# Two layers of a relational graph network on one core: own products per chunk in place of four chunks at once, and rows copied by ScalarE as well as by SyncE

## The chip, the cores and the metric

The kernel runs on one core of a Trainium2 chip. The core has five engines that each work through their own list of instructions in order: TensorE (PE in the profile; its weight loads are shown apart as PEld), VectorE (DVE), ScalarE (ACT), GpSimd (POOL) and SyncE (SP). [...] The metric is the device time of one execution in microseconds (us); lower is better. The kernel before took 22690.96 us (median of three runs, 22663.02 to 22782.8).

## The reference

There are 50,000 nodes with 128 features each, 850,000 edges (800,000 drawn at random in both directions, and one loop per node), 16 relations. Edges come sorted by their target node. One layer is

```python
W = jnp.einsum('rb,bio->rio', w_comp, basis)          # 16 matrices from 8 bases
seg = dst * N_REL + rel
agg = jax.ops.segment_sum(h[src], seg, num_segments=N_ENT * N_REL)
msg = jnp.einsum('nri,rio->no', agg.reshape(N_ENT, N_REL, -1), W)
out = jax.nn.relu(msg + h @ loop_w + bias)
```

Two such layers follow each other, and the result is `layernorm(x + layer2(layer1(x)))`. The bulk of the data traffic is `h[src]`: 800,000 rows of 512 bytes per layer, at random places.

## The kernel before, in words

**Chunks.** The edges that are not loops are laid out in 625 chunks (`C`) of 10 tiles (`K`) of 128 edges, in the order of their target nodes. For every layer the function `chunked` walks the chunks in one long unrolled program. For a tile, 128 source rows are fetched into an SBUF tile `g`, and one matmul (L1023) multiplies them by `hot`, a matrix that VectorE makes (L913) out of the relation weights and the edges' places among the tile's 12 possible targets. Five tiles fill one PSUM bank `pa`; ScalarE copies it to `aT` (L1031, `aT<-pa`, two copies per chunk). There are two `pa` banks.

**Own products.** `aT` holds, for each of 8 bases, 120 target slots of the chunk. It has to be multiplied by the bases. Before, this is done for `BATCH = 4` chunks together: `slots_of_batch` runs 8 matmuls with 480 columns (L754) into `ps`, ScalarE copies the result out (`by_slot`, L760), four matmuls transpose it into `po` (L764), and VectorE spreads each chunk's part over four node positions (`spread_out`, L742). The last chunks (from `ALONE`) go one by one through `slots` (L732).

**Nodes.** `to_nodes` (L796) adds the spread slots to groups of 512 nodes, which are summed in PSUM banks `pn`; this happens `LAG = 6` chunks after the chunk's own matmuls. `from_itself` makes the part of a group that comes from its own loop (L695, L710, L717, L725), and `finish` adds both, applies the nonlinearity and stores the group.

**Fetching rows.** Two paths bring rows. Nearly all tiles come by an indirect gather on GpSimd (L206), one instruction for 128 rows, issued two chunks ahead (`FETCH`) into one of five buffers (`GATHERS`). In every fifth chunk (`BY_HAND = 5`; chunks 9, 14, ... 624, that is 124 per layer) the last tile is instead copied row by row: `row_by_row` loads the 128 offsets from DRAM (`row_at`, L842), SyncE reads them into registers, 32 at a time (L851), and issues one DMA of 512 bytes for each row (L859). The generator starts `BY_HAND + EARLY = 8` chunks ahead of use and is advanced one step after every tile, 45 steps for 128 rows.

**What sets the order.** The program order of PE, POOL, DVE and ACT is the order of the source, held by a manual schedule. The function `beside` puts pieces of the other work after each tile. SyncE's order is left to the scheduler, which follows the source closely. So SyncE issues, in one list: the 128 rows, the `row_at` loads, `rel` (L625: the relations of the next four chunks, on which VectorE waits at L632), `h_own` (L685), `lrel`, `xw`, and the stores of finished groups (L821, L826). In the built program the DMAs issued by SyncE carry one of eight completion semaphores in turn, and a DMA waits until the one that last used its semaphore has landed.

Of the kernel before, what the change touches and what calls it, by code (L numbers as in the profile page):

```python
# [72 lines left out]
BATCH = 4  # L73
BY_HAND = 5
EARLY = 3
OFFSETS = 32
LAG = BATCH + 2
# [8 lines left out]
def tile_rgcn_resnorm(  # L86
# [33 lines left out]
    assert D == P and N >= P and edges.shape[0] == 1 and AT * NR == P and PER * NB * WN <= BANK and AT * PER * NB == WEIGHTS and PER == HALF and S <= P and C >= 4 and M > 0 and N % C == 0 and N % J == 0 and J * D == BANK and C % BATCH == 1 and C > 4 * BATCH and RUN - LK // 2 == LIVE and C <= RUN and 2 * C <= NG * P and N <= 1 << 16 and E % ROW == 0  # L120
# [10 lines left out]
    ROW_AT = dram.tile([2 * C, P], I32, name="ROW_AT")  # L131
# [310 lines left out]
    def rows_of(j, pool):  # L442
# [36 lines left out]
        row_at = pool.tile([P, LIVE], F32, name="real").bitcast(I32)[:, :P]  # L479
        nc.vector.tensor_scalar(row_at[:m], srcf[:m, LIVE - P :], float(N - 1), float(4 * D), op0=OP.min, op1=OP.mult)  # L480
        nc.sync.dma_start(ROW_AT[r0 : r0 + m], row_at[:m])
# [63 lines left out]
    def count_up(pool):  # L545
        last = 5 * NG + len(ROWS)
        off = pool.tile([P, RUN], F32, name="k_f")[0:1, :C]
        even = pool.tile([P, RUN], F32, name="loop_f")[0:1, :C]
# [48 lines left out]
    def chunked():  # L597
        with (
# [7 lines left out]

            ALONE = C - BATCH - 1

# [12 lines left out]
            def weights(c, n):  # L621
# [9 lines left out]
                is_rel = hp.tile([P, LIVE], F32, name="is_rel", bufs=1)  # L631
# [14 lines left out]
            def loop_weights(g, n):  # L646
# [14 lines left out]
                is_rel = rel.bitcast(F32)  # L661
                for h in range(2):
                    nc.vector.tensor_scalar(is_rel[:m, h, :], rel[:m, h, :], its_rel1[:m], None, op0=OP.is_equal)  # L663
                    if h == 0:
                        yield
                po = ps_o.tile([P, BANK], F32, name="po")
                of = po[:, : J * T * NB].rearrange("p (j t) -> p j t", j=J)
                for j in range(J):
                    for h in range(2):
                        nc.tensor.matmul(  # L670
                            of[:, j, :],
                            is_rel[:m, h, :].rearrange("k (p j) -> k p j", j=J)[:, :, j],
                            EACH[n][:m, :T, :].rearrange("k t b -> k (t b)"),
                            start=h == 0,
                            stop=h == 1,
                        )
# [4 lines left out]
            def from_itself(g, of, n):  # L681

                m = nodes(g)
                h = sb.tile([P, J, D], F32, name="h_own", bufs=1)
# [43 lines left out]
            def slots(c, k, aT, n):  # L728
# [7 lines left out]
                yield spread_out(c, ps[:, :D])  # L736

            def spread_out(c, of):

                k = ks(c) * WN  # L740
                st = sb.tile([P, J, D], F32, name="slots", bufs=BATCH)
                nc.vector.tensor_tensor(  # L742
                    st[:k],
                    of[:k, None, :].to_broadcast([k, J, D]),
                    which[:k, c, :, None].to_broadcast([k, J, D]),
                    op=OP.mult,
                )
                return st

            def slots_of_batch(c, aT, st, n):  # L750

                ps = ps_s.tile([P, BANK], F32, name="ps")
                for b in range(NB):
                    nc.tensor.matmul(  # L754
                        ps[:, : BATCH * S], BASIS[n][:, b, :], aT[:, b, :], start=b == 0, stop=b == NB - 1
                    )
                    if b < NB - 1:
                        yield
                by_slot = sb.tile([P, BATCH * S], F32, name="by_slot", bufs=1)
                nc.scalar.copy(by_slot, ps[:, : BATCH * S])  # L760
                yield
                po = ps_o.tile([P, BANK], F32, name="po")
                for q in range(BATCH):
                    nc.tensor.transpose(po[:S, q * P : (q + 1) * P], by_slot[:, q * S : (q + 1) * S], ident)  # L764
                    if q == 1:
                        yield
                for q in range(BATCH):
                    st[c + q] = spread_out(c + q, po[:, q * P : (q + 1) * P])
                    if q == 1:
                        yield  # L770
                yield
# [61 lines left out]
            behind = []  # L833

            def by_hand(c):

                return ks(c) == K and c >= BY_HAND + EARLY and c % BY_HAND == BY_HAND - 1

            def row_by_row(c, of):

                row_at = hp.tile([1, P], I32, name="row_at")
                nc.sync.dma_start(row_at, ROW_AT[2 * c + 1 : 2 * c + 2])  # L842
                to = hp.tile([P, D], F32, name="by_hand")
                byte = of.bitcast(U8).rearrange("n d -> (n d)")
                yield to
                steps = BY_HAND * (K - 1)
                for step in range(steps):
                    for e in range(step * P // steps, (step + 1) * P // steps):
                        if e % OFFSETS == 0:
                            with tc.issue_after(behind[-1]) if behind else ExitStack():  # L850
                                _, offsets = nc.values_load_multi_w_load_instructions(  # L851
                                    row_at[:, e : e + OFFSETS],
                                    engines=[mybir.EngineType.SP],
# [5 lines left out]
                        behind[:] = [nc.sync.dma_start(row, byte[None, ds(offsets[e % OFFSETS], 4 * D)]).ins]  # L859
# [39 lines left out]
            for n, of in enumerate((x, H1)):  # L899
# [21 lines left out]
                def sum_up(c):  # L921
                    at = c % BATCH * S
                    for st[c] in slots(c, ks(c), aTs[c // BATCH][:, :, at : at + S], n):
                        yield

                def added_in(c):

                    if c < ALONE + 2:
                        return [c - LAG] if c >= LAG else []
                    at = ALONE - BATCH + 2 * (c - ALONE - 2)  # L930
# [323 lines left out]
```

## Time and profile before

| | |
|---|---|
| median of three runs | 22690.96 us |
| the profiled execution: its time, its span | 22663.02 us, 22661.2 us |
| PE, weight loads (PEld) busy | 11605.0 us, 7642.6 us |
| POOL busy | 11614.3 us |
| DVE busy, ACT busy | 6712.8 us, 1902.9 us |
| mean granted TensorE clock | 0.717 |
| gathers (L206) | 2 x 6126 |
| row copies (L859) | 2 x 15872 |
| mean DMA rate | 46 GB/s |

The profiled execution is the fastest of the three runs, 28 us (0.1%) under the median. In a line of the profile, `L859` is the line of the kernel, `by_hand<-H` the tile written and the one read, `x15872` the number of instructions, and a wait is listed as total us, number of times, longest. SyncE has no busy time in the profile's own count, since issuing DMAs is not counted as busy; what it does must be read from the starts of its instructions.

### The profile page before, as it was taken

To read this page: it belongs to the slowest core of one execution; us is meant where nothing else is said; L and a number is where in the kernel's file an instruction comes from. 1 tells how busy PE (TensorE), PEld (TensorE's weight loads), DVE (VectorE), ACT (ScalarE), POOL (GpSimd) and SP (SyncE) were. 2 spreads that over 40 slices of the span, in tenths; PEclk is the share of its full clock that TensorE was granted. 3 is DMA by queue.
4 is the path that set the end of the run, shared out by engine and by line. 5 is a ranking of instruction groups with operands and counts; after the bars stand their busy time and mean duration, and the time that the engine had idled before them with its cause. 6 is when DMAs were issued, how large, how long until landed. Compare 5 with 4: busy or idle time off the path is not lost. (4 is left out here: it accounts for less than half of the span.)

```text
span 22661.2 us, 191120 instructions
## 1 busy us (share of the span) xinstructions
PE 11605.0 (51%) x45072; PEld 7642.6 (34%) x45072; DVE 6712.8 (30%) x11506; ACT 1902.9 (8%) x3706; POOL 11614.3 (51%) x12285
## 2 busy tenths in 40 slices
PE   4545444544455554554555555555545555455555
PEld 2333333333333333333333333333333333333333
DVE  3333333333222222222222222222222222222222
ACT  0000000000000000000000000000000000000000
POOL 4544544545455554554555555555545555555554
PEclk7767677777677777776767777777767777777777
DMA  2111111111111111111111111111111111111111
GB/s 58 52 49 50 49 49 45 48 49 50 45 44 46 44 43 43 43 47 41 45 44 46 45 47 45 47 46 44 46 43 48 46 45 47 44 46 46 44 48 41
DMA packets 597898, 1048.67 MB, mean 46 GB/s; under 512 B 242858, under 2 KB 320422, under 8 KB 596762
## 3 DMA queue, kind: packets, MB, share of 16 engines
q0 software_dynamic: 395616, 810.55, 13.7%
q1 hardware_dynamic: 197930, 224.36, 3.1%
q8 instruction: 368, 6.03, 0.1%
q14 instruction: 768, 6.29, 0.1%
q10 hardware_dynamic: 3216, 1.45, 0.0%
HBM read 962.43 MB, written 72.95 MB: 46 GB/s over the span
## 5 line engine op out<-in xcount | busy, mean ns | idle before, releaser
L206 POOL DMA_INDIRECT g<-H,src x6126 | 5791.7, 945 | 5388.5 <-PE pa L1023 2718.1
L206 POOL DMA_INDIRECT g<-in_x_dram,src x6126 | 5796.8, 946 | 5111.4 <-PE pa L1023 2627.1
L1023 PEld LDWEIGHTS pa<-hot,g 128*128 128x128 f32 x24504 | 4553.1, 236 | 4871.2 <-issue 3484.1
L1023 PE MATMUL pa<-hot,g 128*128 128x96 f32 x24504 | 4535.0, 313 | 1929.5 <-ACT aT L1031 1107.3
L754 PE MATMUL ps<-aT,basis 128*128 128x480 f32 x4960 | 3081.3, 707 | 1314.3 <-ACT aT L1031 872.4
L796 PE MATMUL pn<-slots,own 120*128 120x512 f32 x4128 | 2507.0, 730 | 2229.8 <-DVE slots L742 1787.1
L710 PE MATMUL po<-basis,hT 128*128 128x512 f32 x3136 | 2035.6, 736 | 2340.5 <-DVE by L717 2107.8
L1031 ACT COPY aT<-pa 128x480 f32<-128x480 f32 x2500 | 1375.6, 558 | 17880.7 <-remote 9150.3
L717 DVE TENSOR_TENSOR by<-po,lw 128x512 f32<-128x512 f32 x1568 | 1069.9, 687 | 4347.4 <-PE po L710 1638.7
L913 DVE TENSOR_TENSOR hot<-fixed,own 128x960 f32<-128x960 f32 x1250 | 1447.1, 1158 | 1699.0 <-remote 1379.3
L796 PEld LDWEIGHTS pn<-slots,own 120*128 120x128 f32 x4128 | 857.0, 236 | 2792.6 <-DVE slots L742 1806.3
L725 DVE TENSOR_REDUCE ls<-by 128x128 f32<-128x1152 f32 (+1 forms) x784 | 1661.9, 2120 | 34.6 <-DVE by L717 0.4
L632 DVE TENSOR_SCALAR is_rel<-rel,its_rel 128x640 f32<-128x640 uint8 x314 | 176.9, 563 | 4458.7 <-DMA rel<-REL 4277.5
L754 PEld LDWEIGHTS ps<-aT,basis 128*128 128x128 f32 x4960 | 924.1, 231 | 1375.4 <-ACT aT L1031 899.6
L710 PEld LDWEIGHTS po<-basis,hT 128*128 128x128 f32 x3136 | 565.2, 226 | 2413.0 <-DVE by L717 2152.7
L742 DVE TENSOR_TENSOR slots<-po,which 120x512 f32<-120x512 f32 x1240 | 780.7, 681 | 1576.4 <-remote 780.6
L906 DVE TENSOR_TENSOR own<-fixed,key 128x120 bf16<-128x120 f32 x1250 | 344.2, 275 | 1887.7 <-remote 1092.0
L764 PE MATMUL po<-ident,by_slot 128*120 128x128 f32 x1240 | 346.6, 375 | 1039.7 <-ACT by_slot L760 798.4
L670 PE MATMUL po<-each,lrel 64*128 64x32 f32 (+1 forms) x800 | 205.8, 416 | 1106.3 <-DVE lrel L663 1052.0
L695 PE MATMUL po<-ident,h_own 128*128 128x128 f32 (+1 forms) x784 | 189.9, 333 | 934.0 <-DMA h_own<-H 606.6
L670 PEld LDWEIGHTS po<-each,lrel 64*128 64x128 f32 (+1 forms) x800 | 193.7, 324 | 1119.1 <-DVE lrel L663 1063.3
L764 PEld LDWEIGHTS po<-ident,by_slot 128*120 128x120 f32 x1240 | 189.7, 193 | 1087.4 <-ACT by_slot L760 831.0
(140 smaller groups left out, 4025.1 us busy)
## 6 DMA issues: line engine op xcount, KB each, us to landing
by_hand<-in_x_dram SPq DMA_DIRECT2D x15872, 0.5 KB
by_hand<-H SPq DMA_DIRECT2D x15872, 0.5 KB
g<-in_x_dram,src POOLq DMA_INDIRECT x6126
g<-H,src POOLq DMA_INDIRECT x6126
rel<-REL SPq DMA_DIRECT2D x312, 80.0 KB
h_own<-in_x_dram SPq DMA_DIRECT2D x97, 256.0 KB
xw<-in_x_dram SPq DMA_DIRECT2D x97, 256.0 KB
H<-ls SPq DMA_DIRECT2D x97, 256.0 KB
```

The lines of the kernel that those rows point to most:

```text
L206: return nc.gpsimd.indirect_dma_start(out=to, out_offset=None, in_=of, in_offset=bass.IndirectOffsetOnAxis(ap=idx, axis=0))
L670: nc.tensor.matmul(of[:, j, :], is_rel[:m, h, :].rearrange("k (p j) -> k p j", j=J)[:, :, j], EACH[n][:m, :T, :].rearrange("k t b -> k (t ...
L710: nc.tensor.matmul(hb[:m], hT[:, j, :m], BASIS[n][:, b : b + few, :].rearrange("p b d -> p (b d)"), start=True, stop=True,)
L717: nc.vector.tensor_tensor(by[:m, b : b + few, :], hb[:m].rearrange("p (b d) -> p b d", d=D), lw[:m, j, g % T, b : b + few, None].to_broadc ...
L725: nc.vector.tensor_reduce(ls[:m, j, :], by[:m].rearrange("p b d -> p d b"), AX.X, OP.add)
L742: nc.vector.tensor_tensor(st[:k], of[:k, None, :].to_broadcast([k, J, D]), which[:k, c, :, None].to_broadcast([k, J, D]), op=OP.mult,)
L754: nc.tensor.matmul(ps[:, : BATCH * S], BASIS[n][:, b, :], aT[:, b, :], start=b == 0, stop=b == NB - 1)
L764: nc.tensor.transpose(po[:S, q * P : (q + 1) * P], by_slot[:, q * S : (q + 1) * S], ident)
L796: nc.tensor.matmul(sums[g], own, of[:k].rearrange("s j d -> s (j d)"), start=c == first(g), stop=c == final(g),)
L913: nc.vector.tensor_tensor(hot[:, : ks(c)], pm[:, c % Q * K : c % Q * K + ks(c), :, None].to_broadcast([P, ks(c), NB, WN]), own[:, : ks(c), ...
L1023: product = nc.tensor.matmul(pa[:, i * NB * WN : (i + 1) * NB * WN], g[:, k + i, :] if k + i < ks(c) - by_hand(c) else handed.pop(c), hot[ ...
L1031: nc.scalar.copy(aT[:, :, place_of + k * WN : place_of + (k + m) * WN].rearrange("d b (i w) -> d i b w", w=WN), pa[:, : m * NB * WN].rearr ...
```

## The change

It has three parts.

1. The batch goes. `slots_of_batch`, `spread_out`, `by_slot` and the transposes are removed; every chunk now runs `slots`: 8 matmuls of 128 columns with `aT` as the weights, and VectorE spreads directly out of `ps`. `aT` becomes a tile per chunk (three buffers), the sum into nodes comes 3 chunks after the chunk instead of 6, and the steps of `beside` are placed accordingly.
2. The row copies have two hands, `HANDS`. SyncE copies a tile in every fifth chunk as before (124 per layer). ScalarE copies one in every sixth chunk (chunks 8, 14, ... 620: 103 per layer), with its own register loads and its own DMA starts on ScalarE's list; the offsets are still fetched by a DMA of SyncE. Those tiles are no longer gathered, so there are 2 x 6023 gathers. Each hand starts `every + 1` chunks ahead (6 for SyncE, 7 for ScalarE), with 45 and 54 steps. `ROW_AT` holds the offsets of two tiles of each chunk.
3. Buffers: `h_own` and `is_rel` get two each, `is_l` is a tile of its own, two small vectors of `count_up` as well.

In the program built from it, ScalarE's row copies stand between its `aT<-pa` copies, about 2.4 after each tile, and the eight completion semaphores are shared by SyncE's and ScalarE's DMAs in the order of the program.

```diff
-BATCH = 4
-BY_HAND = 5
-EARLY = 3
+SP_EVERY = 5
+ACT_EVERY = 6
...
-    ROW_AT = dram.tile([2 * C, P], I32, name="ROW_AT")
+    ROW_AT = dram.tile([2 * C, 2, P], I32, name="ROW_AT")
...
-                is_rel = hp.tile([P, LIVE], F32, name="is_rel", bufs=1)
+                is_rel = hp.tile([P, LIVE], F32, name="is_rel")
...
-                h = sb.tile([P, J, D], F32, name="h_own", bufs=1)
+                h = sb.tile([P, J, D], F32, name="h_own", bufs=2)
...
-                yield spread_out(c, ps[:, :D])
-
-            def spread_out(c, of):
-
-                k = ks(c) * WN
-                st = sb.tile([P, J, D], F32, name="slots", bufs=BATCH)
+                st = sb.tile([P, J, D], F32, name="slots")
                 nc.vector.tensor_tensor(
-                    st[:k],
-                    of[:k, None, :].to_broadcast([k, J, D]),
-                    which[:k, c, :, None].to_broadcast([k, J, D]),
+                    st[: k * WN],
+                    ps[: k * WN, None, :D].to_broadcast([k * WN, J, D]),
+                    which[: k * WN, c, :, None].to_broadcast([k * WN, J, D]),
                     op=OP.mult,
                 )
-                return st
-
-            def slots_of_batch(c, aT, st, n):
-
-                ps = ps_s.tile([P, BANK], F32, name="ps")
-                for b in range(NB):
-                    nc.tensor.matmul(
-                        ps[:, : BATCH * S], BASIS[n][:, b, :], aT[:, b, :], start=b == 0, stop=b == NB - 1
-                    )
...
-                by_slot = sb.tile([P, BATCH * S], F32, name="by_slot", bufs=1)
-                nc.scalar.copy(by_slot, ps[:, : BATCH * S])
...
-            behind = []
+            behind = {}
+            HANDS = ((nc.sync, SP_EVERY, SP_EVERY - 1), (nc.scalar, ACT_EVERY, ACT_EVERY // 2 - 1))
 
             def by_hand(c):
 
-                return ks(c) == K and c >= BY_HAND + EARLY and c % BY_HAND == BY_HAND - 1
-
-            def row_by_row(c, of):
-
-                row_at = hp.tile([1, P], I32, name="row_at")
-                nc.sync.dma_start(row_at, ROW_AT[2 * c + 1 : 2 * c + 2])
-                to = hp.tile([P, D], F32, name="by_hand")
+                if ks(c) < K:
+                    return []
+                return [i for i, (_, every, at) in enumerate(HANDS) if c > every and c % every == at]
+
+            def row_by_row(i, c, of):
+
+                engine, every, _ = HANDS[i]
+                tile_at = 1 - by_hand(c).index(i)
+                row_at = hp.tile([1, P], I32, name=f"row_at{i}", bufs=2)
+                nc.sync.dma_start(row_at, ROW_AT[2 * c + 1 : 2 * c + 2, tile_at])
+                to = hp.tile([P, D], F32, name=f"by_hand{i}", bufs=2)
                 byte = of.bitcast(U8).rearrange("n d -> (n d)")
                 yield to
-                steps = BY_HAND * (K - 1)
+                steps = every * (K - 1)
                 for step in range(steps):
                     for e in range(step * P // steps, (step + 1) * P // steps):
...
-                                    engines=[mybir.EngineType.SP],
+                                    engines=[engine.engine],
...
-                        behind[:] = [nc.sync.dma_start(row, byte[None, ds(offsets[e % OFFSETS], 4 * D)]).ins]
+                        behind[i] = engine.dma_start(row, byte[None, ds(offsets[e % OFFSETS], 4 * D)]).ins
...
-                        for k in range(ks(to) - by_hand(to)):
+                        for k in range(ks(to) - len(by_hand(to))):
...
-                    to = c + BY_HAND + EARLY
-                    if to < C and by_hand(to):
-                        fetching = row_by_row(to, of)
-                        handed[to] = next(fetching)
+                    for i, (_, every, _) in enumerate(HANDS):
+                        to = c + every + 1
+                        if to < C and i in by_hand(to):
+                            fetching[i] = row_by_row(i, to, of)
+                            handed.setdefault(to, {})[K - 1 - by_hand(to).index(i)] = next(fetching[i])
...
                             if k + i < K - 1:
-                                next(fetching, None)
+                                for each in fetching.values():
+                                    next(each, None)
```

## The prediction, made before the changed kernel was run

> **What bounds the kernel now.** I read the page first. No engine is busy for more than half of the span, so the bound must be a wait, or an engine whose work is not counted.
>
> ```profile
> span 22661.2 us, 191120 instructions
> PE 11605.0 (51%) x45072; PEld 7642.6 (34%) x45072; DVE 6712.8 (30%) x11506; ACT 1902.9 (8%) x3706; POOL 11614.3 (51%) x12285
> ```
>
> Then the longest waits over all engines:
>
> ```profile
> POOL g L206 <- PE pa L1023: 5345.2, 368, 50.1
> DVE is_rel L632 <- DMA rel<-REL: 4277.5, 172, 65.9
> PE po L710 <- DVE by L717: 2107.8, 195, 52.6
> ```
>
> GpSimd waits for TensorE to free a buffer, TensorE for VectorE, and VectorE for `rel`, an 80 KB transfer that SyncE issues. With the DMA engines 17% busy it is late because its issue is. The list of SyncE's own waits says that SyncE itself hardly waits for anybody:
>
> ```profile
> SPq L859 <- DMA by_hand<-H: 171.4, 333, 1.4
> SPq L859 <- DMA by_hand<-in_x_dram: 165.9, 338, 1.4
> SPq L826 <- ACT ls L595: 93.3, 21, 20.4
> ```
>
> It always has something to issue: 31,744 row copies in a span of 22,661 us, one per 0.71 us. The instructions of line L859 in two stretches of 20 us (12016 to 12036, then 12085 to 12105) show that the pace depends on what GpSimd does at that time; the two last lines are the busy time of PE, PEld, DVE, ACT and POOL in the same stretches, then the granted clock, the DMA engines' share and GB/s:
>
> ```profile
> L859 SPq DMA_DIRECT2D by_hand<-H x18: 3/230/700, 12017.3 to 12035.0; - x18
> L859 SPq DMA_DIRECT2D by_hand<-H x46: 2/228/263, 12085.4 to 12104.9; - x46
> 12016.00:12036.00 20.00, 9.89 (x55) 8.12 (x53) 2.49 (x4) 1.12 (x2) 15.12 (x17) 0.67 0.21 53
> 12085.00:12105.00 20.00, 0.00 (x0) 0.00 (x0) 0.00 (x0) 0.00 (x0) 0.19 (x1) 0.50 0.02 5
> ```
>
> 46 rows while GpSimd rests and the engines stand still, 18 beside 17 gathers. I counted the starts of both kinds in all 20 us stretches of the trace. Without a gather SyncE starts 44.2 rows (81 stretches), which is 0.4525 us per row with register loads and other transfers included. Each gather then costs SyncE a toll: 0.62 us in stretches with 8 to 11 gathers, 0.66 with 12 to 14, 0.73 with 15 to 17. Over the whole span: 31,744 x 0.4525 = 14,364 us, and the remaining 8,297 us over 12,252 gathers are 0.677 us each, inside that table. SyncE's list is the bound: it has no slack, and the others stop until it catches up. The profiled time is 22,663 us, 1.8 above its span and 28 under the median.
>
> **The change part by part: SyncE.** It keeps its 31,744 rows and 992 register loads (2.1 us each, inside the 0.4525). It loses the toll of 206 gathers and gains 206 `row_at` loads, issued in 0.234 us each (median of L842): 14,364 + 12,046 x 0.677 (8,158) + 48 = 22,570 us. That is 0.4% less than the span and the floor of the changed kernel, unless the toll itself changes.
>
> **ScalarE.** It gets 2 x 103 x 128 = 26,368 row copies and 824 register loads. No row shows ScalarE issuing rows beside gathers. From below: SyncE's record of a row is a move of 0.03 and a DMA of 0.228 us, one per 0.323 at best, so 8,517 us. From above: SyncE's full price, 26,368 x 0.4525 = 11,932, the toll of 8,158, and ScalarE's own busy time of 1,902.9 less 174.5 for the removed `by_slot` copies: 21,818 us. I take the upper value, the nearest row being the same instruction on the other queue. ScalarE is then 96% full, just under SyncE.
>
> **What the new wait does.** The eight completion semaphores now go round both queues, so that neither can start more than about eight transfers past the other's place in the program; a hand holds about four of them. Behind a stopped SyncE stand `rel`, `h_own` and the stores, and behind a stopped ScalarE the `aT<-pa` copies, for which the next `pa` bank and so TensorE wait. A stop of one hand that outlasts four rows of the other (4 x 0.323 = 1.29 us) stops both. In the trace of before 6,683 gaps between SyncE's rows are longer than that, with 4,414 us above 1.29; they cover 58% of the span. Scaled to ScalarE's rows (26,368/31,744) the excess is 3,667 us. From below this costs nothing (both stop together, since the gathers cause both), from above 3,667. I take the part that falls outside SyncE's own long gaps if they fall independently, 42%: 1,547 us.
>
> **Two issuers at once.** No row shows two engines issuing rows. From below zero: they do not meet. From above each SyncE row meets a whole ScalarE record: 31,744 x 0.228 = 7,238 us; and, should the whole price be that of a shared path, 26,368 x 0.4525 = 11,932. I take the chance meeting: ScalarE is inside a 0.228 record for 26% of the time and SyncE then waits half of one, 0.26 x 0.114 x 31,744 = about 960 us.
>
> [...]
>
> **The other edits.** TensorE: the batch cost 3,081.3 (L754) and 346.6 us (L764); the 20,000 matmul records that replace it cost 26.4 us per 160 in the tail of the kernel, so 3,300 us:
>
> ```profile
> L754 PE MATMUL ps<-aT,basis 128*128 128x480 f32 x4960 | 3081.3, 707 | 1314.3 <-ACT aT L1031 872.4 <-issue 439.8 <-DMA g<-in_x_dram,src 1.4
> L764 PE MATMUL po<-ident,by_slot 128*120 128x128 f32 x1240 | 346.6, 375 | 1039.7 <-ACT by_slot L760 798.4 <-issue 228.3 <-DVE at_i L521 6.2
> L732 PE MATMUL ps<-basis,aT 128*120 128x128 f32 x160 | 26.4, 306 | 1.8 <-DVE slots L742 1.8
> ```
>
> That is a draw, and more weight loads (10,000 pairs for 3,720) lie in TensorE's idle half. At the single record's 306 ns it would be 6,120 us, 2,700 more; TensorE's idle 11,056 us hide that, and if SyncE were no longer the bound it would be part of the price. VectorE's spreading keeps its 1,250 instructions (681 against 691 ns). The shorter lag and the second buffers cost nothing while everybody waits for SyncE. SyncE's tile is now asked for 6 chunks ahead instead of 8, and finished one chunk before use; TensorE stood idle for 13.7 us in all before matmuls on such tiles, and a late one would only be another sign of SyncE's lateness.
>
> **Sum.** 22,570 + 1,547 + 960 = 25,077 us, 10.6% above the profiled execution and 10.5% above the median.
>
> **The rivals.** (1) ScalarE's rows are hidden altogether: cheap ones (8,517 us) never stop SyncE, and the floor stands, 22,570. For it: ScalarE is 8% busy now. Against it: its rows stand in one list with copies that wait for TensorE, and the shared semaphores tie SyncE to that list. (2) Both hands go through one path and rows add: 58,112 x 0.4525 + 8,158 + 48 = 34,500. For it: the toll, which shows that transfers of another engine do slow SyncE. Against it: with no gather in flight SyncE runs at 0.323 us per row, which is its own instruction time, and the DMA engines are 2% busy there. (3) The other side, faster: with ScalarE's rows between the copies the gathers come evenly, about 10 in 20 us instead of bursts of 16 and pauses, and the toll falls from 0.677 to the 0.62 of such stretches: 14,364 + 12,046 x 0.62 + 48 = 21,880, 3.6% under the median. It decides where the saved toll (12,046 x 0.057 = 690 us) is more than the coupling, so where that is under 690. Against it: the coupling above is more than three times that.
>
> **How the numbers follow.** The two queues coupled, 25,080: chance 0.60, with a range of its own of 23,200 to 29,860 (a quarter of the two terms above the floor; the whole coupling with half of the 7,238). Hidden, 22,570: 0.16, of which 0.10 within 0.5% of the median, 0.03 on each side; 0.5% is about what this kernel's runs can tell from no change. Shared path: 0.11. Even gathers: 0.13. Faster 0.16, same 0.10, slower 0.74. The range 22,400 to 30,500 leaves out most of the even and of the shared case.
>
> **What would show it.** Right: SyncE's waits for row transfers grow from 337 us to over 1,000; ScalarE's rows have gaps like SyncE's; the waits of VectorE for `rel` shrink, as TensorE now waits for `aT` copies. L732 near 3,300 us busy shows the draw. Wrong: ScalarE's rows at 0.32 us beside gathers, or a pace without gathers under 0.3 us per row for both hands, or TensorE busy for most of the span, would each take the sum apart.

## The result, and the profile after

The changed kernel takes 23,699 us (median of four runs, 23,696 to 23,734), the kernel before beside it 22,686. The ratio is 1.044, 95% interval 1.041 to 1.047: slower, as forecast, by less than half of the forecast 10.5%. The profiled execution has a span of 23,732 us.

The head of the page after, for the changed kernel (busy us, share of the span, instructions):

```profile
span 23732.1 us, 272570 instructions
PE 12540.1 (53%) x58712; PEld 9692.4 (41%) x58712; DVE 6751.1 (28%) x11506; ACT 1789.2 (8%) x3396; POOL 11417.3 (48%) x12079
```

Its waits over all engines, and then SyncE's own (total us, times, longest):

```profile
POOL g L204 <- PE pa L979: 6798.7, 619, 36.6
ACT aT L987 <- DMA by_hand<-in_x_dram: 6202.8, 840, 49.7
PE pa L979 <- ACT aT L987: 3941.9, 763, 44.8
DVE is_rel L630 <- DMA rel<-REL: 3345.5, 154, 56.3
```

```profile
SPq L836 <- DMA by_hand<-H: 807.6, 898, 9.4
SPq L836 <- DMA by_hand<-in_x_dram: 740.2, 828, 9.6
```

Still no engine is busy for long. The `aT` copies now stand behind row transfers on ScalarE's list (the `ACT aT` line), TensorE waits 3,942 us for those copies where it waited 1,107 before, and GpSimd waits for TensorE. The 1,107 is the last number of TensorE's group in the page of the kernel before:

```profile
L1023 PE MATMUL pa<-hot,g 128*128 128x96 f32 x24504 | 4535.0, 313 | 1929.5 <-ACT aT L1031 1107.3
```

VectorE's wait for `rel` shrank from 4,278 to 3,346. SyncE's waits at its rows (L836, was L859) grew from 337 to 1,548 us, and the longest from 1.4 to 9.6. This is what the prediction asked to see, except that TensorE's own products (L732) take 4,106 us and not near 3,300. What it does not show is that two effects of opposite sign lie in the 4.4%, and that this number belongs to one kind of chip.

**One thing is needed to read what follows.** The runs came to several chips, of two kinds. On one kind, where the prediction's trace and the result were taken, the kernel before takes 22,680 to 22,920 us. On the other it takes 15,496 to 15,509 us, with the same instructions. I call them the slow and the quick chips. All ratios below are against the kernel before on the same chip.

| run | chip | us | ratio (95%) |
|---|---|---|---|
| changed kernel | slow | 23,699 | 1.044 (1.041 to 1.047) |
| no_act_hand | slow | 21,730 | 0.958 (0.956 to 0.960) |
| act_twelfth, act_twelfth_again | slow | 25,143, 25,385 | 1.109 (1.106 to 1.111), 1.108 (1.106 to 1.110) |
| act_burst | slow | 24,077 | 1.050 (1.048 to 1.052) |
| sp_burst | slow | 24,015 | 1.049 (1.048 to 1.051) |
| both_sixth | slow | 23,243 | 1.014 (1.012 to 1.016) |
| sp_tenth_act_sixth | slow | 21,870 | 0.954 (0.952 to 0.956) |
| act_alone | slow | 19,477 | 0.852 (0.850 to 0.854) |
| no_hands | slow | 18,878 | 0.825 (0.824 to 0.827) |
| before_no_rows | slow | 18,780 | 0.828 (0.827 to 0.830) |
| before_tenth | slow | 19,206 | 0.847 (0.845 to 0.848) |
| before_three_buffers | slow | 22,748 | 0.994 (0.993 to 0.996) |
| after_again (the changed kernel) | quick | 16,827 | 1.085 (1.083 to 1.087) |
| no_act_one_buffer | quick | 15,502 | 1.000 (1.000 to 1.001) |
| before_lead_six | quick | 15,494 | 1.000 (0.999 to 1.001) |
| before_by_tile | quick | 15,496 | 1.000 (0.999 to 1.001) |
| before_half_gathers, half_gathers_again | quick | 13,925, 13,928 | 0.899 (0.897 to 0.900), 0.898 (0.897 to 0.900) |

### The profile page after: what moved, and what is told of

Same layout as the page of the kernel before. It is cut to its first block, busy times and chain, and to the rows that moved or that the text cites. A ratio compares the mean times of both kernels' runs of the same rounds, so it can differ in the third digit from the quotient of the medians.

```text
span 23732.1 us, 272570 instructions
## 1 busy us (share of the span) xinstructions
PE 12540.1 (53%) x58712; PEld 9692.4 (41%) x58712; DVE 6751.1 (28%) x11506; ACT 1789.2 (8%) x3396; POOL 11417.3 (48%) x12079
## 5 line engine op out<-in xcount | busy, mean ns | idle before, releaser
L979 PE MATMUL pa<-hot,g 128*128 128x96 f32 x24092 | 5177.6, 329 | 6925.6 <-ACT aT L987 3941.9
L979 PEld LDWEIGHTS pa<-hot,g 128*128 128x128 f32 x24092 | 4711.5, 248 | 8696.4 <-issue 4551.1
L732 PE MATMUL ps<-basis,aT 128*120 128x128 f32 x20000 | 4106.2, 341 | 98.6 <-issue 56.4
L737 DVE TENSOR_TENSOR slots<-ps,which 120x512 f32<-120x512 f32 x1250 | 862.4, 690 | 10311.5 <-remote 6830.1
L732 PEld LDWEIGHTS ps<-basis,aT 128*120 128x120 f32 x20000 | 3483.4, 243 | 113.1 <-issue 66.7
L768 PE MATMUL pn<-slots,own 120*128 120x512 f32 x4128 | 2656.5, 768 | 985.4 <-DVE own L751 918.8
L670 PE MATMUL po<-each,is_l 64*128 64x32 f32 (+1 forms) x800 | 205.9, 418 | 835.3 <-DVE is_l L661 821.2
L670 PEld LDWEIGHTS po<-each,is_l 64*128 64x128 f32 (+1 forms) x800 | 193.5, 324 | 850.5 <-DVE is_l L661 835.0
L751 DVE TENSOR_SCALAR own<-col,node 120x128 f32<-120x128 f32 x2064 | 528.6, 293 | 12.1 <-PE pn L768 12.1
L635 PE MATMUL fixed<-each,is_rel 128*128 128x64 f32 x3140 | 465.6, 298 | 99.9 <-issue 97.6
```

The lines of the kernel that those rows point to most:

```text
L635: nc.tensor.matmul(of[:, :, j * NB : (j + 1) * NB], is_rel[:m, j * P : (j + 1) * P], EACH[n][:m], start=True, stop=True,)
L732: nc.tensor.matmul(ps[: k * WN, :D], aT[:, b, : k * WN], BASIS[n][:, b, :], start=b == 0, stop=b == NB - 1)
L737: nc.vector.tensor_tensor(st[: k * WN], ps[: k * WN, None, :D].to_broadcast([k * WN, J, D]), which[: k * WN, c, :, None].to_broadcast([k * ...
L751: nc.vector.tensor_scalar(own[:k], col4[:k], node4[:k, c : c + 1], float(-g * GN), op0=OP.subtract, op1=OP.is_equal)
L768: nc.tensor.matmul(sums[g], own, of[:k].rearrange("s j d -> s (j d)"), start=c == first(g), stop=c == final(g),)
L979: product = nc.tensor.matmul(pa[:, i * NB * WN : (i + 1) * NB * WN], others.get(k + i, g[:, k + i, :]), hot[:, k + i].rearrange("e b w -> ...
```

## The experiments

### Is SyncE's list the bound? before_tenth, before_no_rows

```diff
-BY_HAND = 5
+BY_HAND = 10
```

> The kernel before with SyncE copying a tile in every tenth chunk, not every fifth: 15,872 rows instead of 31,744, 124 more gathers. Theory A (SyncE bounds): 15,872 x 0.4525 + 12,376 x 0.62 = 14,860 us for SyncE, so that GpSimd's pace of 1.25 us per gather (15,470 us) or TensorE takes over: 15,600 to 18,500 us, at most 0.82 of before. If GpSimd's gathers or TensorE were the bound of the kernel before, it would be 22,600 to 23,000, since there is 1% more to gather.

In before_no_rows `by_hand` returns False, and all tiles are gathered:

> The kernel before with no rows by hand at all, every tile gathered: 12,500 gathers. Theory A: GpSimd's 12,500 x 1.25 = 15,625 us are the floor, 15,700 to 18,500 us with what TensorE adds. If the rows by hand relieve the bound, as they would where GpSimd is it: 2% slower than before, about 23,150.

Half of SyncE's rows gone: 0.847. All gone: 0.828. On a slow chip the rows are the bound of the kernel before, and taking them out gains 17%. Both times lie above the 18,500 us at which the expected ranges end, and 18,780 is some 3,150 over 12,500 gathers at 1.25 us, so the rows are not all that keeps this chip from the pace of the gathers. With half of them left SyncE has time to wait for others; its own waits in before_tenth:

```profile
SPq L821 <- ACT ls L820: 1797.2, 69, 61.1
SPq L826 <- ACT ls L595: 1034.7, 72, 28.1
```

In the kernel before the second of these was 93.3 us. A list that waits up to 61 us for a store's data is no bound any more, which fits that the second half of the rows brings only 2%.

### The change without ScalarE's hand, and with half of it: no_act_hand, act_twelfth

```diff
-            HANDS = ((nc.sync, SP_EVERY, SP_EVERY - 1), (nc.scalar, ACT_EVERY, ACT_EVERY // 2 - 1))
+            HANDS = ((nc.sync, SP_EVERY, SP_EVERY - 1),)
```

> The changed kernel without ScalarE's hand: own products per chunk, second buffers and shorter lag stay, 124 tiles per layer by SyncE as before. Theory A (SyncE's list is the bound in both kernels, and what the change adds is SyncE waiting on the completion semaphores that it now shares with ScalarE's transfers): 22,600 to 22,800 us, ratio 0.995 to 1.005. Rival B (TensorE's own products per chunk are the cost): about 23,650. Rival C (rows on ScalarE's list hold up the aT copies and so TensorE): 22,600 to 22,800 as well; runs with fewer ScalarE rows are to tell C from A.

```diff
-ACT_EVERY = 6
+ACT_EVERY = 12
```

> The changed kernel with ScalarE copying a tile in every twelfth chunk, not every sixth: half its rows, 102 more gathers. Theory A: the 1,014 us that the change added are in proportion to the pairs of transfers, so about 23,200 us. Rival B: 23,650, since the own products are as before. Rival C: between, but TensorE's wait for aT copies (3,942 us) halves as well.

None of the expectations had either result. Without ScalarE's hand the changed kernel is 4.2% faster than before, where the prediction had the remaining edits at nothing. So ScalarE's hand costs 23,699 - 21,730 = 1,969 us. Between the two traces the spans differ by 2,005 us, and 1,607 of these are idle time before SyncE's rows (9,127 us against 7,520). The shorter wait of VectorE for `rel` is no sign of the hand, since it is there without it:

```profile
DVE is_rel L630 <- DMA rel<-REL: 3425.1, 156, 61.2
```

With half of ScalarE's rows the hand costs more, not less: some 3,410. SyncE's waits at its rows, first in no_act_hand, then in act_twelfth:

```profile
SPq L836 <- DMA by_hand<-H: 227.3, 463, 1.4
SPq L836 <- DMA by_hand<-in_x_dram: 217.2, 438, 1.7
```

```profile
SPq L836 <- DMA by_hand<-in_x_dram: 1596.3, 749, 45.2
SPq L836 <- DMA by_hand<-H: 1346.6, 732, 17.0
```

444, 1,548 (the changed kernel) and 2,943 us. A wait of 45 us can't be a row's travel: in the quick trace of the changed kernel (after_again, below) a row's data packet starts 0.64 us after the record of its issue ends (median; 0.95 at 95%). It must be a transfer that ScalarE had not issued. I therefore took from each built program which transfer used a semaphore last before each of SyncE's and ScalarE's transfers, and from the trace when that one was issued (idle time of the queue ahead of transfers whose predecessor was not yet issued when the queue was ready):

```
                     SyncE, behind ScalarE     ScalarE, behind SyncE
changed kernel        601 times, 1,410 us      2,001 times, 3,872 us
act_twelfth_again   1,047 times, 4,612 us        368 times,   528 us
act_burst             586 times, 1,666 us      1,669 times, 3,951 us
sp_tenth_act_sixth    297 times,   492 us      1,363 times, 4,402 us
both_sixth            733 times, 1,370 us      2,544 times, 7,389 us
after_again, quick    359 times,   884 us        290 times,   625 us
```

The two hands do hold each other, and what counts is which of them is the later one. In the changed kernel it is mostly SyncE. With half as many rows ScalarE's hand is the later one: SyncE, whose list is the bound, waits 3,202 us more for it, and ScalarE 3,344 less for SyncE. That fits the higher cost of fewer rows: the listed waits of SyncE's rows grew by 1,395 us from the changed kernel to act_twelfth (1,548 to 2,943), the time by 1,444. The repeat, run for another question, gave the same ratio:

> The changed kernel with ScalarE copying a tile in every twelfth chunk and not in every sixth, for a chip without the stops of 0.7 us (kernel before: 15,500 us). SyncE's list takes 13,914 us there when nothing holds it up, and 2,669 us of waits at its rows come on top with both hands at 5 and 6. If the waits go with the number of ScalarE's rows, they halve: 13,914 + 1,335 = 15,250, and the gathers (12,168 x 1.258 + 58 = 15,365) end the time: 0.99. If they go with the number of SyncE's transfers that follow one of ScalarE's on their semaphore (7,454 instead of 10,144): 13,914 + 1,961 = 15,875, 1.025. If half the rows cost more than all, as on the first chips: over 1.085.

### Each hand by itself: no_hands, act_alone

`HANDS = ()`, and `HANDS` with ScalarE's entry alone:

> The changed kernel with neither hand: all 12,500 tiles gathered, own products per chunk. Theory A (SyncE's row copies bound every kernel that has them in every fifth chunk): as the kernel before without rows, 18,780 us, give or take the other edits: 17,900 to 19,200. If TensorE's own products per chunk cost anything by themselves, it shows here, where SyncE no longer hides it: above 19,200.

> The changed kernel with ScalarE's hand alone, a tile in every sixth chunk, and none by SyncE. Theory A (the price of ScalarE's rows is that SyncE's rows wait for them on the shared semaphores): nearly free without SyncE's rows, at most 500 us over the kernel with neither hand. Rival C (ScalarE's rows delay the aT copies, and TensorE with them): 1,000 to 2,000 us over it, as they cost 1,970 beside SyncE's rows (23,700 against 21,730).

0.825 and 0.852: without SyncE's rows beside them, ScalarE's 26,368 rows cost 599 us, against 1,969 beside them. That is a little over the 500 us of theory A, and under the 1,000 to 2,000 of rival C. And no_hands against before_no_rows (0.825, 0.828) says that the own products chunk by chunk cost nothing when there are no rows: TensorE's 20,000 small matmuls are no burden there, although they are busy for 678 us longer than what they replace (4,106 us against 3,081 and 347).

### Changing the order of the rows: sp_burst, act_burst

One hand's steps are taken at the end of a chunk and not after each tile (SyncE's in sp_burst, ScalarE's in act_burst):

```diff
-                                for each in fetching.values():
-                                    next(each, None)
+                                next(fetching.get(0, iter(())), None)
+                    for _ in range(K - 1):
+                        next(fetching.get(1, iter(())), None)
```

> The changed kernel with SyncE's rows of a chunk (about 26) asked for together at the chunk's end instead of three after each tile; ScalarE's stay after each tile. The shared semaphores then change hands between the queues in blocks. Theory A: SyncE's waits for row transfers (1,548 us) fall below 1,000 and the time to 22,300 to 23,300 us. Rival C: the place of ScalarE's rows before the aT copies is as it was, so 23,600 to 23,800.

> The changed kernel, ScalarE's rows asked for nine steps at a time at the end of each chunk (some 21 rows in a row) and not step by step after each tile. In the built program 7,347 of SyncE's transfers follow one of ScalarE's on their semaphore, not 10,144. Chip without the stops: if the waits go with these, 13,914 + 1,933 = 15,850 us, 1.022 of the kernel before, 6% better than the changed kernel there. If the aT copies behind 21 rows (7 us and more) hold up TensorE and so the gathers instead: 1.085 or more. Chip with the stops: under 1.04 by the first, over it by the second.

sp_burst tells nothing: the scheduler put SyncE's list back, and in the built program some 10,100 of SyncE's transfers follow one of ScalarE's on their semaphore, against some 10,150 in the changed kernel. In act_burst it is some 7,350, yet SyncE's waits at its rows are 1,501 us (1,548), and the ratio is 1.050. The number of such pairs does not set the price.

### Less for SyncE with ScalarE's hand kept: both_sixth, sp_tenth_act_sixth

`SP_EVERY` is 6 and 10 in place of 5.

> The changed kernel with SyncE copying a tile in every sixth chunk, ScalarE too. Chip without the stops: SyncE's list 26,368 rows, some 11,740 us, and waits of 2,400 us leave 1,100 us of room under the gathers, 12,108 x 1.258 + 58 = 15,290 us: 0.987 of the kernel before, the fastest of all if the waits stay in that room. If the two hands in step hold each other up more than that: over 1.0. Chip with the stops: about 0.97.

> The changed kernel with SyncE copying a tile in every tenth chunk, and ScalarE one in every sixth as before. Chip without the stops: SyncE's list needs some 7,500 us, so waits of 2,669 us and more have room in it, and the gathers are the bound: 12,190 x 1.258 + 58 = 15,393 us, 0.993 of the kernel before. If it is ScalarE's list or the aT copies behind its rows that hold everything up: over 1.04. Chip with the stops: 0.85 if SyncE's list is the bound there as the other runs say.

I had 0.97 and 0.85 for the slow chip and measured 1.014 and 0.954. In both_sixth ScalarE waits 7,389 us for transfers that SyncE has not issued, the most in the table, and TensorE 6,395 for `aT` copies; why the same period of both hands should do this was not tested. At a tenth SyncE is not the bound: its list has room, as in before_tenth. Beside that run's 0.847 (which has the batch still) ScalarE's hand costs some 0.107 of 22,900, 2,450 us. By the table above ScalarE waits 4,402 us for transfers that SyncE issues late, and SyncE's list waits for VectorE; the `aT` copies stand behind them. The waits of SyncE and of TensorE in sp_tenth_act_sixth:

```profile
SPq L623 <- DVE own L751: 1290.0, 165, 27.7
```

```profile
PE pa L979 <- ACT aT L987: 4938.0, 800, 46.2
```

So the coupling works both ways: a SyncE with room in its list still holds up ScalarE's copies.

### Where does SyncE's toll come from? before_three_buffers, before_by_tile, before_lead_six, no_act_one_buffer, before_half_gathers

On slow chips the gain of no_act_hand goes with shorter unbroken streams of gathers (in the changed kernel itself only 594 gathers are left in streams of 12 or more). Rows of SyncE per gather interval, by the place of the gather in a stream (starts less than 1.3 us apart), counted from the traces:

```
                      place 0-3   4-7   8-11  12-19   gathers in streams of 12 or more
before, slow             2.21    1.29   0.83   0.54        4,554
no_act_hand, slow        2.27    1.33   0.87   0.56        2,057
three buffers, slow      2.18    1.20   0.91   0.55        3,925
before_lead_six, quick   2.58    2.56   2.29   2.71       11,957
```

Two runs were to break the streams up (before_three_buffers: `GATHERS = 3`; before_by_tile: a gather waits for the matmul that read its own tile, not the whole buffer), one shortens the lead alone (before_lead_six: `EARLY = 1`), one takes the second buffers of `h_own` and `is_rel` out of no_act_hand (no_act_one_buffer), and one leaves out half of the gathers (before_half_gathers):

```diff
-                        for k in range(ks(to) - by_hand(to)):
+                        for k in range(0, ks(to) - by_hand(to), 2):
```

> The kernel before with three gather buffers instead of five, nothing else. Counted from the traces so far: SyncE starts 2.2 rows per gather at the first four of an unbroken stream of gathers, 1.3 at the next four, 0.8 at the next, 0.5 past the twelfth, and the kernel before has 4,554 gathers in streams of twelve or more against 2,057 without the batch. Theory D (own products per chunk gain because they break up the long streams, in which SyncE is slowest): three buffers break them up as well, so 21,500 to 22,300 us, although GpSimd may fetch less far ahead. Rival E (the gain of the change without ScalarE's hand comes from elsewhere): fewer buffers gain nothing, 22,700 to 24,000 us.

> The kernel before, but each gather waits for the matmul that read its own tile of the buffer, not for the last matmul of the whole chunk, so GpSimd gets its tiles back one at a time and its gathers no longer start ten or twenty in a row behind one wait. Theory of the streams (SyncE's toll per gather grows along an unbroken stream of gathers, and the 4% that the changed kernel gained without ScalarE's hand came from shorter streams): gathers in streams of 12 or more fall from 4,554 to under 2,500, the toll from 0.677 towards 0.60, so 14,364 + 12,252 x 0.60 + 48 = 21,760 us or 0.96 of the kernel before (0.94 to 0.98). Rival (the streams are only a sign of something else that the other edits changed): 0.99 to 1.01 though the streams get shorter. If the streams do not get shorter, it tells nothing.

> The kernel before with SyncE's tile asked for six chunks ahead and not eight, as in the changed kernel. If the shorter lead made the 4.2%: 0.95 to 0.97. If the own products made it: 0.99 to 1.01.

> The changed kernel without ScalarE's hand, and with one h_own and one is_rel buffer as before the change. If the second buffers made the 4.2% by which the changed kernel without ScalarE's hand beats the kernel before: 0.99 to 1.01. If they cost and bring nothing, as the prediction had it, and the own products chunk by chunk with the shorter lag made it: 0.95 to 0.97.

> The kernel before with every second gather left out (tiles 1, 3, 5, 7 and the gathered 9 of a chunk use the rows of the tile before them, so half of the source rows are wrong rows); everything else, SyncE's list too, is the same. If the gathers take the time from SyncE: 14,364 us plus some 6,250 gathers at 0.677 or less = 18,600 us at most, 0.82 of the kernel before, and down to 0.71 if shorter streams also cost less each (0.3 us), unless another engine ends the time earlier at about 0.80. If SyncE's pace has another cause (its own waits, its registers, the DMAs of the other data), the time stays over 0.95.

Three buffers hardly shortened the streams (3,925), and the time moved by 0.6%: a time in the range of rival E, and since the streams stayed, no test of theory D. The next four runs had a quick chip, where there is nothing to gain: by_tile, lead_six and one_buffer stand at 1.000. They do not tell what made the 4.2% on slow chips. They tell more. The page of before_lead_six, which is the kernel before with a shorter lead:

```profile
span 15493.1 us, 191205 instructions
PE 12167.7 (79%) x45072; PEld 7350.1 (47%) x45072; DVE 6731.1 (43%) x11506; ACT 1939.6 (13%) x3706; POOL 11646.7 (75%) x12285
POOL 51%; issue 21%; DMA 14%; PE 7%; SPq 6%; DVE 1%; ACT 0%; POOLq 0%; ACTq 0%; DVEq 0%
...
L206 POOL DMA_INDIRECT g<-in_x_dram,src x6126 | 5818.1, 950 | 1898.4 <-issue 1716.0
```

The same gathers in the kernel before on the slow chip:

```profile
L206 POOL DMA_INDIRECT g<-in_x_dram,src x6126 | 5796.8, 946 | 5111.4 <-PE pa L1023 2627.1
```

Each engine is busy for as long as on the slow chip to within 5%, and a gather takes the same (950 ns, 946 there). But here GpSimd's idle time before its gathers is nearly all "issue", time in which it waits for nothing that the profile shows: one gather every 1.258 us, 15,435 us from the first to the last. GpSimd is the bound. SyncE starts 49 rows in 20 us beside 17 gathers (stretch 12016 to 12036), where the slow chip had 18:

```profile
L859 SPq DMA_DIRECT2D by_hand<-H x49: 227/228/267, 12016.8 to 12035.8; - x49
```

TensorE's clock does not make the difference: its mean is 0.717 on the slow chip and 0.835 here, but a matmul of L1023 takes no more time there (313 ns in the mean, 322 here). The first-layer instructions of line L859 (ns, shortest/median/longest), first in the kernel before on the slow chip, then in before_lead_six on the quick one:

```profile
L859 SPq MOVE by_hand<-in_x_dram x15872: 1/29/1425, 52.7 to 11410.7; - x199
L859 SPq DMA_DIRECT2D by_hand<-in_x_dram x15872: 1/227/6430, 52.8 to 11410.8; - x199
```

```profile
L859 SPq MOVE by_hand<-in_x_dram x15872: 29/29/38, 52.9 to 7755.9; - x199
L859 SPq DMA_DIRECT2D by_hand<-in_x_dram x15872: 224/228/1431, 53.0 to 7756.0; - x199
```

A register move takes 29 to 38 ns on the quick chip, every time. On the slow one it took up to 1,425 ns, 4,036 of 31,748 over 0.5 us, and others have records of 1 ns. The record of a move names no semaphore and no transfer, so these stops are not the work of the row. SyncE's rows take 8,838 us longer on the slow chip (19,487 against 10,649): 3,471 of these are longer records, and 5,367 idle time before them, though the profile lists only 337 us of waits at these rows.

Do the gathers cause them? Half of the gathers (6,250 in place of 12,252 of tile `g`) end the time at 13,914 us on the quick chip, with SyncE's list full: rows with the idle time before them 10,628 us, register loads 2,209, all else 1,077. In before_lead_six the rows take 10,649. So 6,002 more gathers cost SyncE's rows 21 us, 0.0035 us each. On a quick chip there is no toll. No run with half of the gathers had a slow chip. The trace of before says that the stops go with the gathers there, and not with TensorE: in its 20 us stretches with at most three gathers but 20 to 60 matmuls SyncE starts 42.5 rows (36 stretches), and with 15 to 17 gathers and under 20 matmuls 9.1 (13 stretches). Whether fewer gathers would mean fewer stops is not shown.

### The change on a quick chip: after_again, half_gathers_again

> The changed kernel again, unchanged, beside the kernel before on the same chip. The last four runs had a chip on which the kernel before takes 15,496 us, not 22,690, and on which SyncE's instructions do not stop for 0.7 us at a time; there GpSimd's gathers, one per 1.258 us from the first to the last, fill the whole span. If the chip is of that kind and SyncE's list is no bound there: 12,066 gathers x 1.258 + 58 = 15,230 us, 0.983 of the kernel before. If the two hands hold each other up there as well: over 1.02. If the chip is like those of the first runs: 1.04 again.

> The kernel before with every second gather left out (tiles 1, 3, 5, 7 and the gathered 9 of a chunk use the rows of the tile before them, so half of the source rows are wrong rows). On a chip like those of the first runs: 0.71 to 0.82 if the gathers take SyncE's time (14,364 us plus 6,250 gathers at 0.3 to 0.677), over 0.95 if SyncE's stops of 0.7 us come whatever GpSimd does. On a chip like that of the last four runs: 0.90 again, where SyncE's rows at 0.44 us each (13,970 us) are the bound.

Both went to a quick chip. The changed kernel is 8.5% slower there. Its page and waits:

```profile
span 16821.3 us, 272570 instructions
PE 11015.5 (65%) x58712; PEld 8492.3 (50%) x58712; DVE 6772.4 (40%) x11506; ACT 1791.3 (11%) x3396; POOL 11457.0 (68%) x12079
```

```profile
PE pa L979 <- ACT aT L987: 3069.4, 1039, 22.1
DVE is_rel L630 <- DMA rel<-REL: 2815.9, 169, 36.6
POOL g L204 <- PE pa L979: 1476.3, 363, 29.4
```

```profile
SPq L836 <- DMA by_hand<-H: 1379.1, 2475, 9.2
SPq L836 <- DMA by_hand<-in_x_dram: 1255.7, 2545, 9.4
```

Here the account is simple. SyncE's list, counted from the end of one instruction to the end of the next, is by that counting the whole span: rows 13,310, register loads 2,205, all else 1,305, together 16,820 us. What matters is where it stands idle: 5,066 us before rows, and some 700 before all else. Against half the gathers, where the list was as full, rows are 2,682 us longer, and of that 2,669 are idle time before them (5,066 against 2,397). The records themselves took 8,244 us against 8,231. So GpSimd, which gathers 206 tiles less, gives up the bound to SyncE, which waits 2,669 us longer for transfers: the two lines list 5,020 waits of 0.52 us on average. Waits for a transfer not yet issued by ScalarE are 884 us of it. The rest are waits for transfers already under way, and the semaphore events of the two traces show why. With SyncE alone (half_gathers_again) a row lands 1.24 us after the start of its issue (median), and its semaphore comes round again after eight rows, 8 x 0.323 = 2.58 us at SyncE's best pace: 28 of 30,419 rows find it still under way. With both hands (after_again) a row lands after 1.55 us, and of the 20,834 rows of SyncE that follow one of its own on a semaphore 10,205 come only four transfers later, 4 x 0.323 = 1.29 us: 6,980 of them wait, 1,051 us in all, and 3,488 of the 10,045 behind a row of ScalarE wait another 1,655. A kernel in which the hands have semaphores of their own was not tried, as the kernel does not choose them.

## Why the prediction was right and wrong

- **SyncE's list is the bound, and does not wait:** right on the slow chips (0.847 and 0.828 with rows removed). On the quick ones the bound is GpSimd until ScalarE's hand comes.
- **Quiet price, 0.4525 us per row:** right to 3%: 13,914 / 31,744 = 0.438 on a quick chip with half of the gathers.
- **The toll, 0.677 us per gather, unchanged, and so a floor of 22,570:** this is a step that failed. Without ScalarE's hand the changed kernel has the same rows and gathers as before and takes 21,730, 840 under that floor, and its toll is (21,727 - 14,364) / 12,252 = 0.601. Nor is it a fixed price of a gather: it is 0.0035 us on a quick chip. On a slow chip the stops go with the gathers (42.5 rows in 20 us at up to three gathers, 9.1 at 15 to 17) and grow along their streams (2.21 rows per gather, then 0.54), so one mean toll need not hold in a kernel with other streams.
- **The other edits at nothing:** wrong by the same 840 us on slow chips, right on quick ones (1.000, with one buffer each of `h_own` and `is_rel`). TensorE's draw was taken at 3,300 us busy (4,106 measured on the slow chip, 3,486 on the quick), and stayed hidden. Which of the edits thins the stops on a slow chip is open; the streams of 12 gathers and more fell from 4,554 to 2,057 with it.
- **ScalarE 96% full, the upper end of 8,517 to 21,818:** too high. Counted along ScalarE's list, its rows take 10,289 us on the quick chip with the idle time before them (7,026 without), near the lower end, and 15,762 on the slow one, waits included. The nearest row had been SyncE's price, which contained the stops.
- **The new wait, 1,547 (0 to 3,667):** the shared semaphores do tie the hands: SyncE's waits for row transfers went over the 1,000 that it named, and TensorE waits for `aT` copies. (`rel` waits shrank as well, but without ScalarE's hand too.) The reason was half right. It took the wait to come from long stops of one hand alone; on the quick chip, where no register move of SyncE's rows takes over 38 ns, it is 2,669, because four rows (1.29 us) no longer cover a row's landing (1.55), and because SyncE meets rows that ScalarE has not issued yet. That its size comes near on the slow chip is in part luck.
- **Two issuers at once, 960:** failed. No run shows the meeting that this term priced: on the quick chip, at one row per 0.53 us from SyncE and one per 0.64 from ScalarE (after_again), the records of SyncE's rows took 13 us more in all than the 8,231 with SyncE alone (before_half_gathers). On the slow chip the second issuer cost 1,969 us over the same kernel without it (no_act_hand), and of the 2,005 us between the two traces 1,607 are idle time before SyncE's rows.
- **The sum:** floor 840 too high; wait and meeting together 2,507 for a measured 1,969, 538 too high. Together 1,378 us, which is 25,077 less 23,699. The time lies inside the range of the coupled case, 23,200 to 29,860, near its lower end. On the quick chip the two terms, 2,507, stand against 2,669, which with the second term at nothing is luck.
- **The rivals:** "hidden" and "shared path" fell. "Even gathers" had a toll that falls to about 0.62 when gathers do not come in long streams. It fell to 0.60, but without ScalarE's rows between the copies; that the shorter streams made it fall is not shown. And the coupling was more than the saving, as was held against it.

## What to carry to other kernels

Before you price an instruction by what it seems to suffer from a neighbour, look at the shortest and longest record of something that has no transfer of its own, like a register move: 29/29/38 ns (before_lead_six, quick) or 1/29/1425 (before, slow) tells whether the queue itself stops. A second engine that issued row copies here shared the completion semaphores with the first, and each then waited for the other's list: keep the copies on one list, and expect that thinning the second one can make it worse (1.108 against 1.044 here). Lists whose other work does not wait might do as well; no run tried that. And see a bound on more than one chip before a tuned split between two engines is believed: here SyncE's rows cost 17% on one kind; on the other, where the kernel before is bound by its gathers, each tile copied by hand in place of a gather should take about 1.258 us out of that bound as long as SyncE's list has room, an estimate from the pace of its gathers.

## What the runs showed of the hardware

- The same kernel takes 22,690 us on some chips and 15,496 on others. In the traces of before (slow) and before_lead_six (quick) no engine's busy time differs by more than 5%. One chip was drawn twice, hours apart, and was slow both times (the kernel before took 22,678 and 22,915 us on it).
- The stops come in steps of about 0.7 us, on moves and on DMA issues alike: in the trace of before 4,036 moves and 4,393 issues of SyncE's rows are over 0.5 us, and of these 8,429 records 7,972 take 0.65 to 0.75 us and 186 take 1.35 to 1.45. They thicken along streams of gathers (rows per gather 2.21 to 0.54 in the table). In the trace of the changed kernel on the slow chip 5% of SyncE's row packets start 1.16 us or more before the record of their issue ends; on the quick chip 99% start at least 0.59 us after it. So at least these stops fall after the transfer has left.
- The slow traces also hold fewer semaphore events: 98,452 for the kernel before, 297,976 for before_lead_six on the quick chip, with nearly the same program, while the instruction records (191,120 and 191,205) and the DMA packets (597,898 and 597,899) agree to within 0.05%. Whether the missing events have to do with the stops is not shown. There is no execution whose records were switched off, so it is open too whether the slow chips are slow without them. What makes the stops stays open.
